# Three small memsets on GpSimd between one indirect transfer and the next, in a kernel of four mixture-of-experts layers

## The chip, the cores and the metric

The kernel runs on one core of a Trainium2 chip. The time is the device time of one execution in microseconds (us); the median of several executions without the profiler is what counts. The engines have short names in the profile: PE is TensorE (PEld its weight loads), DVE is VectorE, ACT is ScalarE, POOL is GpSimd, SP is SyncE, which issues the plain DMAs.

## The reference

Two sequences of 1024 tokens with 256 features, 2048 tokens in all, go through six stages, all in float32, each added to the residual stream x:

```
x = x + 0.5 * moe_L0(layernorm(x))        # 8 experts, 2 per token, width 176, and a shared expert
x = x + rwkv(layernorm(x))                # time mixing and channel mixing
x = x + 0.5 * moe_L0(layernorm(x))        # the same weights again
x = x + 0.5 * moe_L1(layernorm(x))        # 32 experts, 6 per token, width 96, and a shared expert
x = x + linear_attention(layernorm(x))    # per sequence: a sum over its keys and values
x = x + 0.5 * moe_L1(layernorm(x))
```

A mixture-of-experts layer routes each token to its K best experts:

```
scores = softmax(x @ gate_w)  (L0)  or  sigmoid(x @ gate_w)  (L1)
topk_w, topk_i = top_k(scores, K)                 # L1 normalizes the K weights
out = sum over the K experts of  topk_w * (silu(x @ w_gate[e]) * (x @ w_up[e])) @ w_down[e]  +  shared(x)
```

## The kernel before

The residual stream stays in SBUF as 16 tiles of 128 tokens; the first eight are the first sequence (called half 0), the last eight the second (half 1). The kernel is written in a framework that orders every engine's instructions itself: it simulates a timeline with its own costs, takes the instructions in the program's priority as they become ready there, and fixes each engine's order at build time. [...]

A mixture-of-experts layer (`sparse_moe`, L270) runs once for each of the four layers, and has these steps:

- `prep` (L294) normalizes four tiles, transposes them, and computes the routing; `plan` (L326) works out for each token and each of its K experts a slot: a row in a DRAM buffer `xs`, ordered so that each block of 128 rows belongs to one expert. `ready(h)` does both for half h.
- `scatter(h)` (L396) writes the half's normalized tokens to their slots: for each of 8 tiles and each of K experts one indirect DMA of 128 rows of 1 KB, issued by GpSimd (L401). That is 16 in each half of L0 and 48 in each half of L1.
- `shared(h)` (L483) computes the shared expert, `weights(h)` (L430) collects the routing weights.
- `blocks(rate)` (L606) goes over all blocks of slots of both sequences ("joint blocks"): `fetch` (L509) reads a block from `xs` with a DMA on SyncE's queue, `features` (L516) transposes it, `inner` (L535) and `outward` (L555) multiply with the expert's weights, and the result goes to a DRAM buffer `ys` (L568). Every fetch waits for all scatters of the layer, of both halves.
- `combine(h)` (L596) brings the results back: for each tile and k one indirect DMA on GpSimd reads 128 rows of `ys` into a tile `yk` (`gather`, L573, issued at L578; eight such tiles in turn), and four steps later VectorE adds them to x, with their weights (`add_back`, L588, L589). The gathers of half 0 wait only for the blocks that half 0 can use (`first`), so they run beside the remaining blocks; those of half 1 wait for all blocks.

Between the layers lie rwkv (L727, L775), after the first layer, and attention (`attend`, L825), which runs for one sequence beside the gathers of the other. The program's end (L987 to L1035) sets the order: among other things `finish(m0["combine"](1), ready)` stands ahead of `m1["scatter"](0)`; `attend(0)` and `m2["ready"](0)` run beside `m1["combine"](1)`; `m2["scatter"](0)` and `m2["shared"](0)` come before `attend(1)`, and `m2["dispatch"](1)` after it. The last layer is made with `last=True`, which also sends each finished tile to the output.

GpSimd has little else to do: constants at the start, and additions in rwkv (L785, L807). The slots of L1 are filled with zeros by one DMA after the first layer (`fill_slots`, L256).

Of the kernel before, what the change touches and what calls it, by code (L numbers as in the profile page):

```python
# [8 lines left out]
F32 = mybir.dt.float32  # L9
# [5 lines left out]
P = 128  # L15
# [29 lines left out]
def macaron_kernel(ctx: ExitStack, tc: tile.TileContext, a: dict, out: bass.AP):  # L45
    nc = tc.nc
    ctx.enter_context(tc.block(schedule_with_timeline_sim=True))

    const = ctx.enter_context(tc.tile_pool(name="const", bufs=1))
# [26 lines left out]
    row = const.tile([P, 1], F32, name="row")  # L76
# [170 lines left out]
    def load_down(w, layer, lo, n):  # L247
# [5 lines left out]
            ),  # L253
        )

    def fill_slots(xs, n, behind=None):  # L256

        zero = const.tile([P, D], F32, tag="zero", name=f"zero_{n}")
        nc.gpsimd.memset(zero, 0.0)
        d = nc.sync.dma_start(  # L260
            out=xs.rearrange("(n p) d -> p n d", p=P),
            in_=zero.unsqueeze(1).to_broadcast([P, n, D]),
        )
        if behind is not None:
            tc.add_manual_dep(d.ins, behind.name, SYNC, reason="not beside the blocks' loads")
# [4 lines left out]
    def sparse_moe(layer, w, nth, xs, ys, moe, last=False):  # L270

        name = f"{layer}_{nth}"
# [4 lines left out]
        xs, ys = xs[0 : NBLK * P, :], ys[0 : NBLK * P, :]  # L277
# [5 lines left out]
        idx = back.tile([P, NT, K], I32, tag="idx", name=f"idx_{name}", bufs=2)  # L283
# [112 lines left out]
        def scatter(h):  # L396

            for i in range(HT):
                t = HT * h + i
                for k in range(K):  # L400
                    d = nc.gpsimd.indirect_dma_start(  # L401
                        out=xs,
                        out_offset=bass.IndirectOffsetOnAxis(ap=idx[:, t, k : k + 1], axis=0),
                        in_=xn[h][:, i, :],
                        in_offset=None,
                    )
                    tc.declare_no_dep(
                        d.ins, group=f"slots_{name}", reason="a slot is one pair's"
                    )
                    tc.add_to_no_dep_group(f"slots_{name}", d.ins)  # L410
                    scattered.append(d.ins)
# [161 lines left out]
        def gather(t, k):  # L573

            yk = back.tile([P, D], F32, tag="yk", name=f"yk_{name}_{t}_{k}", bufs=8)

            n = first if t < HT else NBLK
            d = nc.gpsimd.indirect_dma_start(  # L578
                out=yk,
                out_offset=None,  # L580
                in_=ys[0 : n * P, :],
                in_offset=bass.IndirectOffsetOnAxis(ap=idx[:, t, k : k + 1], axis=0),
            )
            for s in stored[0:n]:
                tc.add_manual_dep(d.ins, s.name, SYNC, reason="the blocks are done")
            gathered[t, k] = yk
# [9 lines left out]
        def combine(h, lag=4):  # L596

            pairs = [(t, k) for t in range(HT * h, HT * h + HT) for k in range(K)]
            for n in range(len(pairs) + lag):
                if n < len(pairs):  # L600
                    gather(*pairs[n])
                if n >= lag:
                    add_back(*pairs[n - lag])
                yield
# [30 lines left out]
        def dispatch(h):  # L635
            for _ in ready(h):
                pass
            scatter(h)
            if h == 1:
                owners()  # L640

        return dict(
            ready=ready,
            scatter=scatter,
            owners=owners,
            dispatch=dispatch,
# [308 lines left out]
    xs, ys = {}, {}  # L955
# [9 lines left out]
    def rest_of_x():  # L965
        for b in range(1, NB):
            load_x(b)
        fill_slots(xs["L0"], moe_blocks(MOE["L0"]))
# [8 lines left out]
    with tc.tile_pool(name="rwkvw", bufs=1) as weights:  # L977
        with tc.tile_pool(name="moe_L0_0", bufs=1) as pool:
            m = sparse_moe("L0", w0, 0, xs["L0"], ys["L0"], pool)
            m["dispatch"](0)  # L980
            m["dispatch"](1)
            load_rwkv(weights)
            m["shared"](0)
            m["weights"](0)
            m["shared"](1)
            m["weights"](1)
            finish(m["blocks"](2))  # L987
        finish(m["combine"](1))
        fill_slots(xs["L1"], moe_blocks(MOE["L1"]), behind=m["latest"]["add"])
        with tc.tile_pool(name="rwkv", bufs=1) as pool:  # L990
            rw["pool"] = pool
            run(rwkv, False)
# [96 lines left out]
```

## Time and profile before

| | us |
|---|---|
| median of 3 runs (1546.06 to 1552.24) | 1547.15 |
| profiled execution | 1739.74 |
| its span | 1737.5 |
| PE busy | 1202.7 (69%) |
| DVE busy | 758.1 (44%) |
| ACT busy | 578.8 (33%) |
| POOL busy | 523.5 (30%) |
| of that: 256 gathers (L578), 975 ns each | 249.6 |
| of that: 256 scatters (L401), 966 ns each | 247.4 |

The profiled execution is longer than the timed runs, so its times are compared with its own span first. "Busy" is the time in which an engine's instructions run; an arrow `<-` after an idle time names what ended it. "remote" in a timeline and "another core or an unknown queue" in the chain stand for a release that the profile could not assign; "issue" is time in which an engine waited for nothing that the profile shows. The chain is followed back from the last instruction to what released it, step by step. The granted clock of TensorE was 0.817 of full speed on average.

### The profile page before, as it was taken

Reading aid. Unit: us, or ns where it says so; the run is one execution under the profiler, and the core shown is the slowest. Engines: PE = TensorE matmul, PEld = TensorE weight load, DVE = VectorE, ACT = ScalarE, POOL = GpSimd, SP = SyncE. Lnnn points to the kernel's source line nnn. Section 1 sums busy time; section 2 is a strip of 40 time slices with the busy share of each in tenths; the row PEclk is TensorE's granted clock in tenths of the full one; section 3 lists DMA queues with packets and bytes.
Section 4 is the critical chain, followed back from the end, with each engine's and each line's share of the span. In section 5 each row is a group of like instructions: output and inputs, shape, how many; then the busy total and the mean of one; then the engine's idle time right before and its main releaser. Section 6 shows DMA issues by size and latency. Waiting matters only on the chain.

```text
span 1737.5 us, 20794 instructions
## 1 busy us (share of the span) xinstructions
PE 1202.7 (69%) x5462; PEld 907.0 (52%) x5462; DVE 758.1 (44%) x2588; ACT 578.8 (33%) x1552; POOL 523.5 (30%) x559
## 2 busy tenths in 40 slices
PE   6589867899976997510629996874734726997730
PEld 4467643566664775410418995742522515996630
DVE  5322349665243234412604444657705712444543
ACT  2123335776331333400105662421302203663310
POOL 1500222111124003175460006446171072004546
PEclk8699978899967998855759998986866767998975
DMA  9502327400082033542124665632030024666743
GB/s 273 179 27 92 119 85 254 157 1 1 1 186 82 25 104 118 134 142 78 52 103 123 188 186 176 205 92 85 22 106 18 8 104 140 185 188 183 210 133 107
DMA packets 182907, 203.01 MB, mean 117 GB/s; under 512 B 40044, under 2 KB 165772, under 8 KB 182796
## 3 DMA queue, kind: packets, MB, share of 16 engines
q1 hardware_dynamic: 158220, 134.55, 25.8%
q0 software_dynamic: 24576, 67.14, 12.3%
q8 instruction: 50, 0.82, 0.2%
q14 instruction: 61, 0.50, 0.1%
HBM read 100.68 MB, written 100.93 MB: 116 GB/s over the span
## 4 chain that ended last, share of the span: by engine, by line
PE 56%; DVE 11%; another core or an unknown queue 11%; issue 10%; DMA 5%; POOL 3%; ACT 2%; SPq 2%; POOLq 0%; DVEq 0%; ACTq 0%
PE pg_L_b L542 15%; PE py_L_b L559 10%; PE pg_L L454 5%; PE px_L L520 4%; PE py_L L496 4%; PE pkk_cm L705 3%; PE pkv_cm L717 3%; PE ph_L_b L470 3%; DMA yk_L<-ys_L,idx_L 3%; POOL xs_L L401 2%; DVE x L589 2%; PE lg_L L305 1%; PE ph_L L470 1%; DMA ys_L<-yb_L 1%
## 5 line engine op out<-in xcount | busy, mean ns | idle before, releaser
L578 POOL DMA_INDIRECT yk_L<-ys_L,idx_L x256 | 249.6, 975 | 715.1 <-DMA ys_L<-yb_L 418.2
L401 POOL DMA_INDIRECT xs_L<-xn_L,idx_L x256 | 247.4, 966 | 281.5 <-DVE idx_L L394 152.3
L445 DVE TENSOR_TENSOR h_L_b<-g_L_b,pg_L_b 128x96 f32<-128x96 f32 (+1 forms) x332 | 90.1, 271 | 334.5 <-ACT g_L_b L444 290.7
L542 PE MATMUL pg_L_b<-L1gu,xbT_L 128*128 x1016 | 215.9, 337 | 4.9 <-issue 3.4
L520 PE MATMUL px_L<-ident,xb_L 128*128 128x128 f32 x664 | 132.1, 282 | 79.8 <-DMA xb_L<-xs_L 46.6
L542 PEld LDWEIGHTS pg_L_b<-L1gu,xbT_L 128*128 128x128 f32 x1016 | 165.8, 197 | 24.0 <-issue 5.4
L589 DVE SCALAR_TENSOR_TENSOR x<-yk_L,wk_L,x 128x256 f32<-128x256 f32 x256 | 121.7, 478 | 96.9 <-DMA yk_L<-ys_L,idx_L 81.3
L559 PE MATMUL py_L_b<-L1down,hT_L_b 96*128 x508 | 157.1, 392 | 9.3 <-ACT hT_L_b L477 7.1
L567 DVE COPY yb_L<-py_L_b 128x256 f32<-128x256 f32 x332 | 140.0, 422 | 52.3 <-PE py_L_b L559 18.3
L444 ACT ACTIVATE g_L_b<-pg_L_b 128x96 f32<-128x96 f32 (+1 forms) x332 | 88.5, 266 | 206.2 <-PE pg_L_b L542 146.2
L520 PEld LDWEIGHTS px_L<-ident,xb_L 128*128 128x128 f32 x664 | 93.4, 145 | 110.4 <-DMA xb_L<-xs_L 47.0
L524 ACT COPY xbT_L<-px_L 128x256 f32<-128x256 f32 x332 | 123.0, 371 | 63.7 <-issue 51.1
L477 ACT COPY hT_L_b<-ph_L_b 96x128 f32<-96x128 f32 (+1 forms) x332 | 95.3, 287 | 130.2 <-PE ph_L_b L470 55.8
L123 PE MATMUL pt_L<-ident,xn_L 128*128 128x128 f32 x128 | 26.2, 350 | 121.1 <-DVE xn_L L115 103.4
L542 PE MATMUL pg_L_b<-L0gu,xbT_L 128*128 x312 | 107.7, 468 | 0.0
L470 PE MATMUL ph_L_b<-ident,h_L_b 128*96 128x128 f32 (+1 forms) x410 | 101.6, 279 | 3.6 <-issue 3.1
L454 PE MATMUL pg_L<-L0sgu,xTs_L 128*128 128x352 f32 x256 | 93.4, 501 | 2.0 <-DVE h_L L445 2.0
L559 PE MATMUL py_L_b<-L0down,hT_L_b 88*128 x312 | 83.1, 389 | 13.5 <-issue 8.2
L559 PEld LDWEIGHTS py_L_b<-L1down,hT_L_b 96*128 96x128 f32 x508 | 83.1, 197 | 11.9 <-ACT hT_L_b L477 8.6
L123 PEld LDWEIGHTS pt_L<-ident,xn_L 128*128 128x128 f32 x128 | 19.3, 182 | 127.3 <-issue 120.1
L445 DVE TENSOR_TENSOR h_L<-g_L,pg_L 128x176 f32<-128x176 f32 (+1 forms) x96 | 31.9, 340 | 122.5 <-ACT g_L L444 74.3
L559 PEld LDWEIGHTS py_L_b<-L0down,hT_L_b 88*128 88x128 f32 x312 | 60.4, 196 | 35.0 <-issue 9.7
(216 smaller groups left out, 1849.5 us busy)
## 6 DMA issues: line engine op xcount, KB each, us to landing
xb_L<-xs_L SPq DMA_DIRECT2D x332, 128.0 KB
ys_L<-yb_L SPq DMA_DIRECT2D x332, 128.0 KB
xs_L<-zero SPq DMA_DIRECT2D x1, 16256.0 KB
xs_L<-zero SPq DMA_DIRECT2D x1, 4992.0 KB
xs_L<-xn_L,idx_L POOLq DMA_INDIRECT x256
yk_L<-ys_L,idx_L POOLq DMA_INDIRECT x256
L1gu<-in_L_gate SPq DMA_DIRECT2D x8, 384.0 KB
L1gu<-in_L_up SPq DMA_DIRECT2D x8, 384.0 KB
```

Of the source, the lines that this page charges most:

```text
L401: d = nc.gpsimd.indirect_dma_start(out=xs, out_offset=bass.IndirectOffsetOnAxis(ap=idx[:, t, k : k + 1], axis=0), in_=xn[h][:, i, :], in_o ...
L445: nc.vector.tensor_tensor(dst, g, pg[:, width : 2 * width], ALU.mult)
L454: nc.tensor.matmul(pg, xT[half][:, c, i * P : (i + 1) * P], w["sgu"][:, c, u, :, :].rearrange("p z w -> p (z w)"), start=(c == 0), stop=(c ...
L470: nc.tensor.transpose(pt[0:m, k * P : (k + 1) * P], h[:, r : r + m], ident)
L477: nc.scalar.copy(hT[0:m, lo:hi, :].rearrange("p k t -> p (k t)"), pt[0:m, lo * P : hi * P])
L520: nc.tensor.transpose(px[:, c * P : (c + 1) * P], xb[:, c * P : (c + 1) * P], ident)
L524: nc.scalar.copy(xbT.rearrange("p c t -> p (c t)"), px[:, 0 : DC * P])
L542: nc.tensor.matmul(pg, xbT[:, c, :], w["gu"][:, c, bass.ds(e, 1), :, :].rearrange("p e z h -> p (e z h)"), start=(c == 0), stop=(c == DC - 1),
L559: nc.tensor.matmul(py, hT[0:HP, k, :], w["down"][:, bass.ds(e, 1), k, :].rearrange("p e d -> p (e d)"), start=(k == 0), stop=(k == C - 1),)
L567: nc.vector.tensor_copy(yb, py)
L578: d = nc.gpsimd.indirect_dma_start(out=yk, out_offset=None, in_=ys[0 : n * P, :], in_offset=bass.IndirectOffsetOnAxis(ap=idx[:, t, k : k + ...
L589: added = nc.vector.scalar_tensor_tensor(x[t], gathered.pop((t, k)), wk[:, t, k : k + 1], x[t], ALU.mult, ALU.add)
```

## The change

A tile `pause` of 128x128 float32 is made. A new function `spaced` wraps the issue of an indirect transfer: after the transfer it puts three memsets of that tile on GpSimd, and the next transfer of the same group (the scatters of one half of one layer, or the gathers of one layer) is ordered behind the last of them. `tc.issue_after(i)` orders what is issued inside it behind instruction i on the same engine, without a semaphore. All scatters are wrapped, and all gathers except those of the last layer.

```diff
+    pause = const.tile([P, P], F32, tag="pause", name="pause")
+
+    pauses = {}
+
+    def spaced(of, d):
+
+        if of in pauses:
+            with tc.issue_after(pauses[of]):
+                d = d()
+        else:
+            d = d()
+        with tc.issue_after(d.ins):
+            for _ in range(3):
+                pauses[of] = nc.gpsimd.memset(pause, 0.0).ins
+        return d
+
...
                 for k in range(K):
-                    d = nc.gpsimd.indirect_dma_start(
+                    d = spaced(("xs", name, h), lambda: nc.gpsimd.indirect_dma_start(
                         out=xs,
                         out_offset=bass.IndirectOffsetOnAxis(ap=idx[:, t, k : k + 1], axis=0),
                         in_=xn[h][:, i, :],
                         in_offset=None,
-                    )
+                    ))
...
             n = first if t < HT else NBLK
-            d = nc.gpsimd.indirect_dma_start(
-                out=yk,
-                out_offset=None,
-                in_=ys[0 : n * P, :],
-                in_offset=bass.IndirectOffsetOnAxis(ap=idx[:, t, k : k + 1], axis=0),
-            )
+
+            def row():
+                return nc.gpsimd.indirect_dma_start(
+                    out=yk,
+                    out_offset=None,
+                    in_=ys[0 : n * P, :],
+                    in_offset=bass.IndirectOffsetOnAxis(ap=idx[:, t, k : k + 1], axis=0),
+                )
+
+            d = row() if last else spaced(("yk", name), row)
```

## The prediction

> **What bounds the kernel now.** I read the page's chain first, then GpSimd's groups, then the busy time by stage, and last the chain and the timelines in the stages where GpSimd is busy.
>
> The page, the chain by engine, and the two groups that the change touches:
>
> ```profile
> PE 56%; DVE 11%; another core or an unknown queue 11%; issue 10%; DMA 5%; POOL 3%; ACT 2%; SPq 2%; POOLq 0%; DVEq 0%; ACTq 0%
> ...
> L578 POOL DMA_INDIRECT yk_L<-ys_L,idx_L x256 | 249.6, 975 | 715.1 <-DMA ys_L<-yb_L 418.2
> L401 POOL DMA_INDIRECT xs_L<-xn_L,idx_L x256 | 247.4, 966 | 281.5 <-DVE idx_L L394 152.3
> ```
>
> TensorE carries the chain, GpSimd seems to carry 3%. But there is one core and no other, and 11% waits for something unknown. Busy time by stage:
>
> ```profile
> core 0: us, PE busy (x) PEld busy (x) DVE busy (x) ACT busy (x) POOL busy (x), PEclk, DMA share, GB/s
> 110.00:200.00 90.00, 90.00 (x427) 68.60 (x426) 26.04 (x69) 32.05 (x106) 0.00 (x0) 1.00 0.24 76
> 730.00:815.00 85.00, 5.63 (x24) 5.12 (x24) 15.46 (x60) 4.22 (x6) 61.72 (x64) 0.50 0.45 140
> 846.00:908.00 62.00, 27.25 (x92) 16.57 (x90) 12.24 (x34) 6.87 (x17) 46.48 (x48) 0.67 0.29 102
> 1145.00:1212.00 67.00, 38.14 (x98) 20.25 (x96) 45.10 (x136) 10.13 (x34) 47.83 (x48) 0.75 0.32 93
> 1249.00:1310.00 61.00, 25.02 (x85) 16.18 (x83) 4.39 (x11) 5.22 (x13) 46.14 (x48) 0.70 0.29 101
> 1385.00:1447.00 62.00, 15.08 (x58) 10.10 (x56) 11.24 (x32) 4.81 (x11) 46.50 (x48) 0.61 0.29 101
> ```
>
> Where the blocks run without indirect transfers (first row) TensorE is busy without a gap. Where indirect transfers run, TensorE is mostly idle. Why it is idle differs (chain, in order of time; then single instructions):
>
> ```profile
> 752.47 29.34 issue
> ...
> 1275.06 41.67 another core or an unknown queue
> ...
> 1441.48 2.37 DMA xs_L<-xn_L,idx_L
> ```
> ```profile
> 781.50 0.28 ACT L157 ACTIVATE s_L<-lg_L 128x128 f32<-128x128 f32 x1 [27.25 <-remote]
> ...
> 1316.71 0.69 DVE L854 TENSOR_TENSOR qk_at<-pqk_at,bc_b_in 128x512 f32<-128x512 f32 x1 [41.65 <-remote]
> ```
>
> At 752 us ScalarE stands 27 us though the logits it needs were finished at 756; at 1275 us VectorE stands 42 us though its product was ready. Both sit inside runs of 48 to 64 indirect transfers. At 1385 us it is different: the third row of the chain is the end of 48 scatters in a row, and the blocks' first read waits for the last of them.
>
> **Profiled time and median.** The profiled execution took 1739.74 us (span 1737.5, 2.2 around it), the median is 1547.15: 192.6 apart. The share of the unknown is 10.6% of the span, 184 us. The stages without indirect transfers run TensorE at full clock without gaps, so the excess cannot be there. I infer that these stalls belong to the profiled execution and are nearly absent in the timed ones. A check: without them the stage from 846 to 925 would end about 46 us earlier (the scatters alone need 846 to 908, and could start at 814), 1249 to 1385 about 50, and the runs at 40 to 95, 200 to 225, 508 to 556, 664 to 690, 1053 to 1212 and 1571 to 1650 about 10, 16, 14, 22, 25 and 12. Sum 195, so 1739.7 - 195 = 1545. So I reckon in a timeline without stalls and make the sum against the median.
>
> [...]
>
> ```profile
> 1.48 0.19 POOL masks.py:65 MEMSET before<- 128x128 f32 x1
> 1.62 0.19 POOL L84 MEMSET every<- 128x128 f32 x1
> 1.77 0.30 POOL L259 MEMSET zero<- 128x256 f32 x1
> ...
> 1250.50 0.98 POOL L401 DMA_INDIRECT xs_L<-xn_L,idx_L  x1 [0.30 <-issue]
> 1251.78 0.96 POOL L401 DMA_INDIRECT xs_L<-xn_L,idx_L  x1 [0.30 <-issue]
> ```
>
> A 128x128 memset spans 0.19 us but starts 0.14 to 0.15 apart; a transfer starts 1.26 after the one before. [...]
>
> **The change part by part.** Nothing is removed. Added: a 64 KB tile (no transfer, no wait) and three memsets after each of 256 scatters (L401) and of 32 + 32 + 96 = 160 gathers (L578); the last 96 gathers stay as they are. That is 416 x 3 = 1248 memsets. Each has no wait on another engine; behind it on GpSimd's queue stands only the next transfer. The ordering edges are within GpSimd and hold each run in the program's order.
>
> Price of a pause, d: 3 x 0.145 = 0.43 us. Below: if the 0.30 between two transfers is preparation that can go on beside the memsets, 0.14. Above: three spans of 0.20 without overlap, 0.60. I take 0.43; 416 x 0.43 = 180 us of GpSimd time. What of it lies on the path, run by run:
>
> 1. L0 scatters (four runs of 16, 37 to 91 and 508 to 555): +7 us each. The first block transpose (L520) is at 131 and 593, 38 us after the scatters' end; the shared experts (L454, L496) cover it. 0.
> 2. L0 gathers of the first half (201 to 221, 664 to 684): 16 x 1.69 = 27 us, beside 16 more blocks, which take about 30 without stalls. 0.
> 3. L0 gathers of the second half, first layer (250 to 271): 16 d = 7 us more; time mixing of the first blocks goes on beside them on a nearly full VectorE (18 of 22 us). Half: 3.5. The large fill of the slots behind the last add moves 7 us later; its slots are wanted at 742 only.
> 4. L0 gathers of the second half and L1's scatters, 730 to 813 (64 transfers) and 846 to 907 (48). Without stalls the 33rd transfer (the last gather) is issued at 773, its add is done at 777, routing and planning take some 31 us (813 to 845 in the trace), so the second half's slots are known at 808, GpSimd is done with its 64 at 814: it is the bound, and stays it (64 d against 33 d). TensorE's shared experts, some 40 us, fit beside. Exposed: 112 d = 48 us.
> 5. L1 gathers of the first half (1044 to 1120, 48): they keep the blocks' pace, 76 us for 60 of transfers; 48 x 1.69 = 81. About 5 late, beside the blocks' last 20 us. 0; without that cover 5.
> 6. L1 gathers of the second half (1145 to 1211): attention of the first sequence runs beside them, VectorE already waits for some (45 of 67 us busy), and its order is fixed. 48 d = 21, half exposed: 10.
> 7. L1's second scatters: the first 48 (1249 to 1310) become 82 us beside attention of the second sequence, which needs about 80 without stalls: 0 (up to 8 if attention is shorter). The last 48 (1385 to 1446) hide behind nothing, TensorE has 15 us of 62: 48 d = 21.
>
> Sum 3.5 + 48 + 10 + 21 = 82.5; 1547 + 82 = 1629 us. At d = 0.14 the sum is 27 (1574); at 0.60 it is 115, and 1678 with items 5 and 7 uncovered.
>
> Memsets also enter the planner's simulated timeline, which orders every engine's instructions; I book nothing, and 20 us either way in the range.
>
> **Rivals.**
> *Faster.* The stalls are real in timed runs too, and pauses let whatever is blocked drain: the stalls begin only some 10 transfers into a run, which speaks for a backlog. It decides from 82 us of stall removed. If all 184 us were there and went, 1547 + 82 - 184 = 1445. Against it: the 192.6 us between profile and median leave no room for them.
> *Hidden.* Preparation in the sequencer covers the memsets wholly, or the pauses fill waits: then 1547. Against it: three starts of memsets alone take 0.43, more than the gap of 0.30, and the last scatters have no cover.
> *Slower still.* Gathers late by the whole of items 2, 3, 5, 6 and 7 hold VectorE in its fixed order, another 40 us, or the planner's order gets worse: 1690.
> That the memsets are dropped as unread is a fifth case; then 1547 as well.
>
> **How the numbers follow.** Slower as summed 0.76 (1560 to 1685), slower still 0.07, faster 0.12, hidden or dropped 0.05. A measurement of this kernel tells about 0.5% from no change. So faster 0.12, same 0.05, slower 0.83. The range 1560 to 1685 takes in both ends of d and the planner, and leaves out faster, hidden and half of slower still, 0.2.
>
> **What the changed profile would show.** Three memsets between two transfers, starts of transfers 1.6 to 1.8 us apart (d), and the last 96 gathers still at 1.25. The last scatters before the second L1 blocks, 61 us now, should take some 82, and still be the chain. Items 1 and 2: the first block transposes at the same distance from the stage's start. The profile itself may well get shorter than 1739.74 while the timed runs get longer[...]; the unknown share would fall below 11%. The prediction is wrong if timed runs contain the stalls (then the median falls), if d is near the gap's 0.1, or if the 730 to 907 stage has another bound, such as planning of the second half ending after 814 us.

## The result, and the profile after

The changed kernel takes 1697.04 us (median of 4 runs, 1695.79 to 1700.36) where the kernel before takes 1547.24: a ratio of 1.0965 [1.0935, 1.0994], so 150 us slower. The forecast was 1629, slower by 82, with 1685 as the upper end. The sign was right, the size was not.

The profiled execution took 1695.79 us with a span of 1694.0, so this time the profile and the timed runs agree. Before they lay 193 us apart. The page of the changed kernel, the chain by engine and GpSimd's three groups:

```profile
PE 43%; POOL 21%; DMA 15%; DVE 9%; issue 8%; ACT 2%; SPq 2%; POOLq 0%; DVEq 0%; ACTq 0%
...
L596 POOL DMA_INDIRECT yk_L<-ys_L,idx_L x256 | 248.7, 971 | 564.5 <-DMA ys_L<-yb_L 428.6
L417 POOL DMA_INDIRECT xs_L<-xn_L,idx_L x256 | 252.2, 985 | 85.5 <-issue 43.5
L269 POOL MEMSET pause<- 128x128 f32 x1248 | 263.0, 211 | 48.5
```

GpSimd had 3% of the chain and has 21%. The transfers themselves take nearly as long as before, 971 and 985 ns each where they took 975 and 966. The 1248 memsets take 263 us, more than either group of transfers, where the prediction reckoned 180 for them. The share of the unknown is gone. GpSimd's timeline, first among the last scatters before the second L1 blocks, then among gathers of the first L1 layer, then among the last gathers, which have no pause (start, duration, instruction, idle time before it):

```profile
1405.68 0.74 POOL L269 MEMSET pause<- 128x128 f32 x3
1406.59 0.97 POOL L417 DMA_INDIRECT xs_L<-xn_L,idx_L  x1 [0.16 <-issue]
1407.56 0.74 POOL L269 MEMSET pause<- 128x128 f32 x3
1408.46 0.97 POOL L417 DMA_INDIRECT xs_L<-xn_L,idx_L  x1 [0.16 <-issue]
...
1120.05 0.95 POOL L596 DMA_INDIRECT yk_L<-ys_L,idx_L  x1 [0.50 <-issue]
1121.00 0.74 POOL L269 MEMSET pause<- 128x128 f32 x3
1122.24 1.20 POOL L596 DMA_INDIRECT yk_L<-ys_L,idx_L  x1 [0.50 <-DVE st_at L109]
...
1606.34 0.95 POOL L596 DMA_INDIRECT yk_L<-ys_L,idx_L  x1 [0.30 <-issue]
1607.59 0.95 POOL L596 DMA_INDIRECT yk_L<-ys_L,idx_L  x1 [0.30 <-issue]
```

Three memsets take 0.74 us, 0.25 each, where the prediction reckoned 0.145. The gap ahead of a scatter falls from 0.30 to 0.16, so a pause adds 0.74 - 0.14 = 0.60; from start to start a scatter takes 1.87 instead of 1.26, so 0.61. Ahead of most gathers the gap grows to 0.50 instead, and a gather takes 2.19 instead of 1.25: 0.94. (Others keep the short gap and take 1.86, among them the first eight of a layer, which find free `yk` tiles.) Busy time by stage:

```profile
core 0: us, PE busy (x) PEld busy (x) DVE busy (x) ACT busy (x) POOL busy (x), PEclk, DMA share, GB/s
729.00:909.00 180.00, 43.80 (x172) 31.99 (x172) 33.55 (x130) 13.42 (x34) 148.90 (x372) 0.59 0.20 71
1150.00:1242.00 92.00, 57.64 (x218) 37.77 (x217) 62.32 (x237) 21.79 (x49) 69.00 (x170) 0.80 0.21 61
1244.00:1334.00 90.00, 57.84 (x240) 40.52 (x238) 66.61 (x262) 23.02 (x63) 76.02 (x182) 0.82 0.19 67
1334.00:1425.00 91.00, 0.00 (x0) 0.00 (x0) 0.00 (x0) 0.00 (x0) 76.01 (x193) 0.50 0.20 69
```

Between 1334 and 1425 us no other engine runs but GpSimd. All the work that used to lie beside the last scatters was done by then. From the first L1 gather at 1029 to the last L1 scatter at 1422 GpSimd never stands still for more than 1.6 us at a time.

One thing has to be known to read the experiments: each of their five sets has its own runs of the kernel before, and these took 1544 to 1547 us in four sets, which I call quiet, and 1729 us in one, which I call stalled. So an execution as long as the profiled one of before is also met among timed runs, and then in all seven of a set.

### The profile page after: what moved, and what is told of

Its sections match the earlier page's. It is cut to its first block, busy times and chain, and to the rows that moved or that the text cites. A ratio compares the mean times of both kernels' runs of the same rounds, so it can differ in the third digit from the quotient of the medians.

```text
span 1694.0 us, 22013 instructions
## 1 busy us (share of the span) xinstructions
PE 1157.9 (68%) x5462; PEld 884.4 (52%) x5462; DVE 761.1 (45%) x2588; ACT 578.4 (34%) x1549; POOL 790.4 (47%) x1807
## 4 chain that ended last, share of the span: by engine, by line
PE 43%; POOL 21%; DMA 15%; DVE 9%; issue 8%; ACT 2%; SPq 2%; POOLq 0%; DVEq 0%; ACTq 0%
DMA yk_L<-ys_L,idx_L 12%; PE pg_L_b L558 11%; POOL xs_L L417 10%; POOL pause L269 8%; PE py_L_b L575 7%; PE pg_L L470 4%; PE pkk_cm L725 3%; PE pkv_cm L737 3%; PE px_L L536 3%; POOL yk_L L596 3%; PE py_L L512 3%; PE ph_L_b L486 2%; DVE x L609 2%; DMA ys_L<-yb_L 1%; PE lg_L L321 1%
## 5 line engine op out<-in xcount | busy, mean ns | idle before, releaser
L417 POOL DMA_INDIRECT xs_L<-xn_L,idx_L x256 | 252.2, 985 | 85.5 <-issue 43.5
L269 POOL MEMSET pause<- 128x128 f32 x1248 | 263.0, 211 | 48.5
L558 PE MATMUL pg_L_b<-L1gu,xbT_L 128*128 x1016 | 213.6, 334 | 2.4 <-PE ph_L_b L486 1.7
L575 PE MATMUL py_L_b<-L1down,hT_L_b 96*128 x508 | 152.8, 382 | 0.2 <-DVE yb_L L583 0.2
L558 PE MATMUL pg_L_b<-L0gu,xbT_L 128*128 x312 | 105.5, 461 | 1.1 <-PE ph_L_b L486 0.6
L470 PE MATMUL pg_L<-L0sgu,xTs_L 128*128 128x352 f32 x256 | 88.2, 478 | 2.0 <-DVE h_L L461 2.0
L486 PEld LDWEIGHTS ph_L_b<-ident,h_L_b 128*96 128x96 f32 (+1 forms) x410 | 49.4, 125 | 34.5 <-DVE h_L_b L461 23.1
```

The source lines that it names most:

```text
L269: pauses[of] = nc.gpsimd.memset(pause, 0.0).ins
L417: d = spaced(("xs", name, h), lambda: nc.gpsimd.indirect_dma_start(out=xs, out_offset=bass.IndirectOffsetOnAxis(ap=idx[:, t, k : k + 1], a ...
L470: nc.tensor.matmul(pg, xT[half][:, c, i * P : (i + 1) * P], w["sgu"][:, c, u, :, :].rearrange("p z w -> p (z w)"), start=(c == 0), stop=(c ...
L486: nc.tensor.transpose(pt[0:m, k * P : (k + 1) * P], h[:, r : r + m], ident)
L558: nc.tensor.matmul(pg, xbT[:, c, :], w["gu"][:, c, bass.ds(e, 1), :, :].rearrange("p e z h -> p (e z h)"), start=(c == 0), stop=(c == DC - 1),
L575: nc.tensor.matmul(py, hT[0:HP, k, :], w["down"][:, bass.ds(e, 1), k, :].rearrange("p e d -> p (e d)"), start=(k == 0), stop=(k == C - 1),)
```

## The experiments

**How much of the pause.** ("Pitch" in the expectations is the time from the start of one transfer to the start of the next.) The same kernel with fewer memsets, with three narrow ones that write columns of their own, and with three narrow ones that all write the same columns. The last two differ only in whether a memset has to wait for the write of the one just before it.

```diff
 # one_memset
-            for _ in range(3):
+            for _ in range(1):
 # three_slices
-            for _ in range(3):
-                pauses[of] = nc.gpsimd.memset(pause, 0.0).ins
+            for n in range(3):
+                part = pause[:, 42 * n : 42 * n + 42]
+                pauses[of] = nc.gpsimd.memset(part, 0.0).ins
 # one_slice: as three_slices, but
+                part = pause[:, 0:42]
 # only_l0, in spaced()
+        if not (of[1].startswith("L0")):
+            return d()
```

> One memset after each transfer instead of three. Pitch theory (every wrapped transfer that lies on the path costs its longer pitch): the memset takes 0.25 us with its wait and the gap before the next transfer shrinks from 0.30 to 0.16, so 0.11 us more per scatter, and up to 0.45 for a gather that has a second wait of its own: 1565 to 1605 us. Planner theory (the memsets make the planner order the engines badly, the memsets' own time matters little): near the changed kernel, 1650 or more. Profile: if the stalls of unknown origin come from profiling of densely issued transfers, the profiled execution exceeds the median by something between 0 and 190 us.

> Three memsets on three separate slices of 42 columns, so that none of the three waits for another. If the price of a pause was missed because each memset waits for the end of the one before (same tile), these three start about 0.06 us apart and the pitch grows by 0.1 us only: 1560 to 1600 us. If the number of memsets after a transfer sets the price, waits or not: above 1630.

> Three memsets of 42 columns, all on the same slice, so that each waits for the one before. Wait theory: some 0.17 us each, pitch 0.35 to 0.4 us longer than before, 1625 to 1650 us, clearly above the version with separate slices, which writes as much. If the written size sets the price: the same as with separate slices.

> Pauses in the two L0 layers alone (64 scatters, 64 gathers). The prediction's items 1 to 3 with its price give 3.5 us, plus 16 gathers of item 4, 7 us: 1558. Pitch theory with the measured pitch: the 32 gathers behind the last block cost 0.6 to 0.95 each, 20 to 28 us: 1567 to 1575. The scatters cost nothing in either.

Measured, against a kernel before of 1729.22 us (1721.63 to 1736.07, 7 runs), in the stalled set: one memset 1672.02, ratio 0.9676 [0.9634, 0.9719]; three slices 1641.62, 0.9494 [0.9418, 0.9571]; one slice 1669.88, 0.9652 [0.961, 0.9694]; pauses in L0's layers alone 1710.68, 0.9879 [0.9832, 0.9926]. The forecasts had reckoned with a kernel before of 1547 us, so their microseconds can't be compared with these; pauses in L0 alone, which were to test items 1 to 3, don't test them. All four are faster than the kernel before, the last by 1% only, which no sum of costs explains. GpSimd's timelines of one memset, three slices and one slice, in this order:

```profile
44.01 0.22 POOL L269 MEMSET pause<- 128x128 f32 x1
44.40 0.97 POOL L417 DMA_INDIRECT xs_L<-xn_L,idx_L  x1 [0.17 <-issue]
```
```profile
45.37 0.29 POOL L270 MEMSET pause<- 128x42 f32 x3
45.83 0.97 POOL L418 DMA_INDIRECT xs_L<-xn_L,idx_L  x1 [0.16 <-issue]
```
```profile
45.32 0.53 POOL L270 MEMSET pause<- 128x42 f32 x3
46.00 0.97 POOL L418 DMA_INDIRECT xs_L<-xn_L,idx_L  x1 [0.15 <-issue]
```

Three memsets of the same size take 0.29 us on columns of their own and 0.53 on the same columns: there they start 0.06 to 0.07 us apart, here 0.19 to 0.21. So the wait for the write before makes these pauses dearer, by 0.24.

The stalls shrink as the transfers move apart. The chain of one memset still has 31% of "issue" and some of the unknown; that of one slice looks like a kernel without stalls. The chain of one memset by engine, its two longest unknown waits (engine and line, us in total, times, longest), and the same of one slice:

```profile
PE 55%; issue 31%; DVE 4%; DMA 4%; SPq 2%; ACT 2%; another core or an unknown queue 1%; POOL 1%; POOLq 0%; DVEq 0%; ACTq 0%
```
```profile
ACT hT_L L493 <- remote: 46.7, 7, 12.3
ACT axT_at L919 <- remote: 40.4, 7, 17.2
```
```profile
PE 48%; POOL 15%; DMA 13%; DVE 10%; issue 8%; ACT 3%; SPq 1%; another core or an unknown queue 1%; POOLq 0%; DVEq 0%; ACTq 0%
```
```profile
ACT g_L_b L461 <- remote: 9.9, 3, 4.0
ACT hT_L_b L494 <- remote: 8.5, 3, 3.8
```

For one slice these two lines are all that there is, 18 us; for one memset all such waits come to 203. This set left open what the pauses cost without stalls, which the next sets answer.

**Which pauses.** The pause in one group of transfers alone, each in `spaced`:

```diff
 # only_scatter_l1_0
+        if not (of[:2] == ("xs", "L1_0")):
+            return d()
 # only_gather_l1_0:   of == ("yk", "L1_0")
 # only_scatter_l1_1:  of[:2] == ("xs", "L1_1")
```

> Pauses in the 96 scatters of the first L1 layer alone. Prediction's item 4 with the measured pitch (1.88 us against 1.26): 96 x 0.62 = 60 us, 1607. If planning of the second half is the bound there, 48 x 0.62 = 30 us, 1577.

> Pauses in the 96 gathers of the first L1 layer alone. The prediction booked half of the second 48 (items 5 and 6), 10 us at its price. Pitch theory: at 2.2 us the 96 gathers take 210 us, VectorE waits for each in its fixed order and attention with it: 40 to 60 us, 1587 to 1607. If the gathers hide beside blocks and attention: below 1560.

> Pauses in the 96 scatters of the last L1 layer alone. Prediction's item 7: the first 48 hide beside attention, the last 48 lie bare: 48 x 0.62 = 30 us, 1577. If the first 48 lie bare too: 60 us, 1607.

Measured, against 1546.64 us (1540.57 to 1551.09): first L1 scatters 1607.23, ratio 1.0388 [1.0355, 1.042], so 60.6 us; first L1 gathers 1619.09, 1.0477 [1.0448, 1.0506], 72.5 us; second L1 scatters 1581.55, 1.0237 [1.021, 1.0264], 34.9 us. The profiles of all three have no unknown wait.

The first is 96 x 0.61 = 59, the whole price of every pause: GpSimd is the bound of that stage, and planning of the second half, the rival here, is not. The third is the same 59 less the 24 us in which GpSimd stands still between the two halves of these scatters where they have no pauses (with pauses in the first L1 scatters alone one starts at 1249.4 and the next at 1274.4, less 1.26); where they have them, the second half starts 2.4 us after the last of the first. The second is the largest single piece, above its forecast of 40 to 60 us, and the prediction had it at 10. With slow gathers GpSimd's queue was also built in another order: the last seven gathers stand among and behind the first half of the second L1 scatters. Its windows from 950 to 1285 us, in three pieces (columns as above):

```profile
950.00:1145.00 195.00, 139.66 (x624) 102.11 (x623) 127.28 (x444) 62.17 (x195) 143.04 (x353) 0.83 0.39 117
1145.00:1219.00 74.00, 19.87 (x81) 13.08 (x79) 19.69 (x57) 8.30 (x25) 57.70 (x77) 0.66 0.29 98
1219.00:1285.00 66.00, 42.05 (x164) 29.51 (x165) 47.81 (x202) 14.47 (x36) 1.11 (x4) 0.76 0.01 2
```

In the second piece GpSimd works nearly alone (VectorE 20 of 74 us); in the third the others work and GpSimd has nothing to do for 66 us, 42 more than the 24 above. So I read the larger part of this kernel's loss as cover that the new order lost; no run separates it from the pauses. The three single losses (168 us) do not simply add up in the changed kernel.

**The pause again, in a quiet set.**

> The changed kernel as it is, again, beside the kernel before on one chip. Two theories of the 183 us between the two times that the kernel before has shown (1547 and 1729 us). Chip theory: some chips (or some condition of a chip) stall the other engines while indirect transfers are issued 1.26 us apart, and a pitch of 1.88 us removes the stalls: about 1697 us on either chip, so slower by 9 to 10% where before takes 1547, faster by 2% where it takes 1729. Recording theory (the prediction's: the stalls belong to executions that are recorded in more detail): the changed kernel would move with the kernel before.

> One memset per transfer (measured pitch 1.35 us). Where before takes 1547: path theory, 150 us for 0.62 us of pitch, so 0.09 gives 22 us: 1569. Where before takes 1729: again near 1672.

> Three short memsets without waits between them (measured pitch 1.41 us). Where before takes 1547: 0.15 of 0.62, 36 us: 1583. Where before takes 1729: again near 1642.

> Three short memsets that wait for one another (measured pitch 1.65 us for scatters, 2.05 for gathers). Where before takes 1547: 0.39 of 0.62, 95 us: 1642, and up to 1670 as on the other chip, since without stalls nothing but the pitch should set it. Where before takes 1729: again near 1670.

Measured, against 1545.31 us (29 runs): the changed kernel 1698.46, ratio 1.0983 [1.0946, 1.102]; one memset 1550.74, 1.0032 [1.002, 1.0044]; three slices 1555.23, 1.0061 [1.0047, 1.0076]; one slice 1652.47, 1.0695 [1.0645, 1.0745]. The one-memset, three-slices and one-slice kernels are those of the first set; what made them 3 to 5% faster there makes them 0.3 to 7% slower here. Both sets together, with the time from one scatter to the next and all unknown waits of the stalled profile added up over the engines (so what overlaps is counted twice):

| | scatter to scatter | quiet | stalled | difference | unknown waits, stalled |
|---|---|---|---|---|---|
| before | 1.26 | 1545 | 1729 | 184 | 294 (first profile) |
| one memset | 1.35 | 1551 | 1672 | 121 | 203 |
| three slices | 1.41 | 1555 | 1642 | 86 | 109 |
| one slice | 1.65 | 1652 | 1670 | 17 | 18 |
| three memsets | 1.87 | 1698 | not run | | |

What the stalled set costs falls with every step by which the transfers move apart, and the unknown waits fall with it. This set was quiet, so it could not show whether the changed kernel moves with the kernel before. Against the recording theory speaks that the profiled executions are as long as the others here: 1698.2 us for the changed kernel in the quiet set, and 1668.42 for one memset in the stalled one.

The quiet column doesn't rise evenly. One memset and three slices cost 5 and 10 us, where the forecasts in proportion to the pitch had said 22 and 36; one slice, at 0.39 (0.79 for a gather), costs 107. Why the small pauses are so cheap was not tested by a run of its own: a part can lie in time in which GpSimd stood still, and a part seems to be made up by the order that the planner built. With three slices the stretch from the first L1 gather to the last L1 scatter takes 318 us, ten less than with pauses in the first L1 scatters alone, though it has pauses and that one has none there.

**A pause without a price.** Memsets of one column: one for each transfer, and three on columns of their own. They keep the ordering of the changed kernel and nearly no time of it.

```diff
 # tiny_one
-            for _ in range(3):
-                pauses[of] = nc.gpsimd.memset(pause, 0.0).ins
+            pauses[of] = nc.gpsimd.memset(pause[:, 0:1], 0.0).ins
 # tiny_slices
+            for n in range(3):
+                pauses[of] = nc.gpsimd.memset(pause[:, n : n + 1], 0.0).ins
```

> The pause is one memset of a single column, so it costs GpSimd about 0.1 us and takes back about as much of the 0.30 us that lie between two transfers: a pitch of 1.22 to 1.32 us against 1.26. Theory (the loss of the changed kernel is pitch times the transfers on the path, the rest is the planner's new order): where the kernel before takes about 1546, 1538 to 1555 (ratio 0.995 to 1.006). Theory that the mere new order of the work costs: over 1570. Where the kernel before takes about 1729: the stalls go with the pitch, so they stay, 1690 to 1735.

> The pause is three memsets of one column each, on columns of their own, so that none waits for the one before. Pitch 1.3 to 1.45 us, as with three slices of the full width (1.41), if a memset's time is mostly fixed; 1.26 to 1.32 if its width counts. Where the kernel before takes about 1546: 1545 to 1560 (ratio 0.999 to 1.009). Where it takes about 1729: 1640 to 1690, as the stalls shrink with the pitch.

> The changed kernel as it is, once more, for the chip it falls on. Where the kernel before takes about 1546: 1697, ratio 1.097. Where it takes about 1729 (theory: the stalls come from transfers at a short pitch and are gone at 1.88 us): again 1695 to 1710, so faster than the kernel before there, ratio 0.98. Rival (that chip stalls whatever the pitch): 1800 or more there.

Measured, against 1545.2 us (39 runs): tiny_one 1539.06, ratio 0.9955 [0.9942, 0.9969]; tiny_slices 1539.3, 0.9966 [0.9954, 0.9979], below its forecast of 1545 to 1560; the changed kernel 1696.64, 1.0977 [1.0931, 1.1023]. GpSimd's timeline of tiny_one:

```profile
38.59 0.97 POOL L416 DMA_INDIRECT xs_L<-xn_L,idx_L  x1 [0.18 <-issue]
39.55 0.12 POOL L268 MEMSET pause<- 128x1 f32 x1
39.86 0.96 POOL L416 DMA_INDIRECT xs_L<-xn_L,idx_L  x1 [0.19 <-issue]
```

From start to start it is 1.27 here and 1.265 in the median of all scatters, the same as in the kernel before; the memset lies wholly in the gap of 0.30. So this pause of 0.12 us costs nothing, and tying the transfers to each other doesn't either. The order that the planner built for the changed kernel is a different one again (it has a scatter among the last gathers of the first L1 layer, tiny_one has none there), and no run has that order without its pauses. In tiny_slices the second L1 scatters start 28 us after the last gather, against 34 to 38 in the kernels with pauses in one group of L1 scatters alone, so the order that is built there is a little better. Both are slightly faster than both kernels of the comparison, by 0.3 to 0.4% of the kernel before. In which stage tiny_one gains its 6 us is not known.

**The sign under stalls.** Whether the changed kernel would be faster in a stalled set is the question of the last set.

> The changed kernel as it is. If it falls on a chip where the kernel before takes about 1729: theory (stalls come with transfers at a short pitch, and are gone at 1.88 us) 1695 to 1710, faster than the kernel before there, ratio 0.98; rival (the stalls of that chip are there whatever the pitch) 1800 or more. Where the kernel before takes about 1546 nothing new: 1697.

> Three memsets of one column each, pitch 1.31 us. If it falls on a chip where the kernel before takes about 1729: the stalls fell from the 1.26 of the kernel before to the 1.41 of three full-width slices by 5.1%, and to the 1.35 of one memset by 3.2%; on that line 1.31 gives about 1.8%, so 1690 to 1710. Where the kernel before takes about 1546: 1539 again, ratio 0.995 to 0.998.

It was quiet: before 1543.97, the changed kernel 1696.55, ratio 1.0972 [1.0946, 1.0998]; tiny_slices 1537.43, 0.9947 [0.9924, 0.997]. It ran on a chip with the same number as the stalled set's, so that number alone doesn't decide it. The changed kernel was never measured in a stalled set. The table suggests about 1700 there (one slice lost only 17 us at 1.65, and this kernel's transfers lie further apart), some 2% faster than 1729; that is an estimate.

## Why the prediction was right in sign and wrong in size

The starts of GpSimd's transfers tell where the 150 us arise. The unchanged parts are read from the kernels with one pause (the first three rows from that with pauses in the second L1 scatters, the last two from that with pauses in the first), the changed kernel from the first quiet set that has it:

| from one start to another | before | changed | more |
|---|---|---|---|
| begin, to the last 16 L0 gathers | 677.9 | 691.9 | 14.0 |
| on to the last scatter of the first L1 layer | 143.3 | 216.0 | 72.7 |
| on to the first L1 gather (the blocks) | 124.9 | 125.2 | 0.3 |
| first L1 gather to last scatter of the second L1 layer | 327.7 | 391.0 | 63.3 |
| on to the last gather | 263.1 | 263.1 | 0 |

The sum is 150.3; the four quiet comparisons of the two kernels gave 150 to 153.

**The price d: the term that failed.** The prediction took 0.43 from memsets at the kernel's start that each fill another tile, 0.145 apart. The pause clears one tile three times, and in the profile of the changed kernel 1246 of the 1248 memsets wait on a semaphore that only GpSimd's own instructions raise: within a pause each starts 0.06 us after the end of the one before, and three take 0.74 us, 0.25 each; that such a wait has a price of its own the slices show, with 0.29 for three memsets against 0.53. The prediction had booked no such wait. Measured, d is 0.61 for a scatter, a hair above the upper bound of 0.60, and 0.94 for most gathers, for which the prediction had no separate price at all.

The trace tells which gathers pay 0.94. In the profile of the changed kernel all 118 gathers with the gap of 0.50 have two waits: one for VectorE, and one for an earlier transfer, which stands as an instruction of its own ahead of them on GpSimd's queue. The 34 without that second instruction have the short gap. In three slices 121 gathers have the same two waits and the short gap. So the long gap needs both, the two waits and the dependent memsets. Such a gather starts 0.70 us after the start of the last memset, whether this one writes 128 columns (gap 0.50) or 42 (gap 0.57). Why that is so isn't known.

**Item 4: right but for d.** It claimed that GpSimd is the bound from 730 to 907 us and that 112 pauses lie open. About 8 of its 16 gathers have the long gap: 8 x 0.94 + 104 x 0.61 = 71, and 72.7 was measured; the scatters alone gave 60.6.

**Items 1 to 3.** The scatters of L0 cost next to nothing, as said. Item 3's half was about right: its 16 pauses are 15 us, and behind them the next layer's scatters start 5 us late. Item 2 was called covered, with 27 us of gathers beside 30 of blocks. In the second L0 layer the gathers take 32 (628.7 to 659.2, and the last one), so the cover is used up, and from their start to that of the second half's gathers it is 63.2 us instead of 56.7: 6.5 late. In the first layer it is 2.5.

**Items 5 to 7: 31 forecast, 63 measured.** The prediction looked at each run of transfers by itself. For item 7 this was nearly right: with the measured price 48 x 0.61 = 29, and 34.9 was measured with pauses there alone. The cover of items 5 and 6 was not: 72.5 us with pauses there alone, where they had 10, or 21 at the measured price.

For the changed kernel the whole stretch can be counted. From the first L1 gather to the last L1 scatter the kernel before needs 327.7 us, of which its 192 transfers take 192 x 1.26 = 242, so GpSimd stands still for 86. The changed kernel needs 391: 82 gathers at 2.19, 14 at 1.86 and 96 scatters at 1.87 make 385. Its pauses come to 82 x 0.94 + 110 x 0.61 = 144; they use up the idle time, and 58 are left over of the 63. The windows of that stretch in the changed kernel of the quiet set and in the kernel with pauses in the first scatters alone show nearly the same work of the other engines beside a GpSimd that has become the bound:

```profile
1033.00:1425.00 392.00, 215.75 (x924) 154.91 (x922) 205.22 (x733) 89.58 (x266) 309.50 (x765) 0.76 0.30 93
```
```profile
1006.00:1336.00 330.00, 217.47 (x927) 155.61 (x925) 204.29 (x734) 93.85 (x270) 189.26 (x192) 0.79 0.36 111
```

The idle time is the most that pauses can hide, not what they do hide. In one slice the pauses of this stretch come to about 109 us and it is 40 longer, not 23; 13 us of the idle time were left. So the sum fits the changed kernel because there no idle time is left, and it would not have given the size from the kernel before alone.

With the measured prices in the prediction's own items 3 to 7 (15 / 2 for item 3, 71 for item 4, half of 41 x 0.94 + 7 x 0.61 for item 6, and 48 x 0.61 for item 7) the sum is 129, so 1676, inside its range. So the price d explains 47 of the 68 us missed, and the remaining 21 are in the main the covers of items 2, 5 and 6 that ran out.

**The stalls.** Two claims stood in the part on the profiled time. That the kernel without stalls takes 1545 was right: 1544 to 1547 in every quiet set. The profile of before also bears out that the excess is not in the blocks without transfers: from 110 to 200, 565 to 660, 925 to 1040 and 1460 to 1570 us TensorE is busy for 409.7 of 410 us at a clock of 1.00, without an unknown wait. That the stalls belong to the profiled execution was wrong: in one set all seven runs of the kernel before took 1722 to 1736. That 193 us lie between profile and median only shows that the two came from different conditions. That the base was right all the same was luck: the changed kernel was compared in the quiet condition. In the stalled set even the sign might have been the other: the four kernels measured there were all faster than the kernel before.

**The rivals.** *Faster* (pauses let a backlog drain) named an effect that exists, with the right sign in the stalled set: three slices gain 5.1% there. In the profile of before the first unknown wait of over 3 us begins 5 to 17 transfers into its run; whether a backlog is behind it isn't shown. It needs the stalls, which the measured comparison didn't have. *Hidden* holds for the pause of 0.12 us in tiny_one. *Slower still* at 1690 had about the right size, but named VectorE held in its order, or a worse order, where the windows above show GpSimd as the bound.

**What the profile was to show.** Scatters 1.6 to 1.8 us apart: 1.87. The last gathers still at 1.25: right. The last 48 scatters 82 us and on the chain: 90 us, and on it, with the 48 ahead of them. The first block transposes of the two L0 layers come 82 and 70 us after the first scatter in the changed kernel of the quiet set and 83 and 69 with pauses in the second L1 scatters alone, so at the same distance, as said. That the profiled time would shrink from 1739.74 came true (1695.79), but it can't be put down to the change: in quiet sets other kernels have no unknown waits either.

## What to carry to other kernels

Price an instruction by a row with the same dependence on what stands before it, not only the same shape: three narrow memsets took 0.29 us here when independent and 0.53 when each waited for the one before, and full-width ones 0.145 each against 0.25. Where one engine has work all through a stretch, add up its work and its idle time over the whole stretch: what goes beyond the idle time is lost (58 us of pauses by that sum, where 63 were measured), and what stays below it may be lost too (59 us of pauses cost 35 in the second L1 scatters, because only 24 of the idle time lay between these). And when a profile and its timed runs differ by a tenth, time the kernel before again beside every experiment before asking what the difference is.

## What the runs showed of the hardware that was not expected

- The same kernel took 1544 to 1547 us in four sets of timed runs and 1729 in one. In stalled executions ScalarE and VectorE wait up to 44 us for releases that the profile can't name, the longest of them in the kernel before from inside runs of indirect transfers, and less in sum the further these lie apart (294, 203, 109, 18 us at 1.26, 1.35, 1.41, 1.65). Pauses in L0's transfers alone left 220 us. What brings a stalled set about was not found.
- A short memset between two indirect transfers takes back 0.11 to 0.15 us of the 0.30 between them, so in tiny_one the memset of a single column was free.
- Behind memsets that wait for one another, a gather with two waits starts 0.70 us after the start of the last memset, whatever its width; behind independent ones the gap ahead of it is 0.16.
